# Splitting PSUM between exponentiated scores and maxima in a causal-attention kernel

## The chip, the cores and the metric

The kernel runs on one core of a Trainium2 chip. The metric is the device time of one execution in microseconds (us). A core has five engines that run side by side: TensorE (PE, matmuls; PEld is its loading of weights), VectorE (DVE), ScalarE (ACT), GpSimd (POOL) and SyncE (SP, which here issues most DMAs). Matmuls write to PSUM, which has 8 banks of 512 float32 columns by 128 partitions. "Bank" below is one of these, a "double bank" two in a row.

## What is computed

A transformer layer on 4096 tokens of width 256, in float32. Causal self-attention with 16 heads of 16 channels comes first, then three feed-forward blocks. All weights carry low-rank additions that the kernel folds in.

```python
qkv = lora_linear(x, w_attn, b_attn, la_attn, lb_attn)
q, k, v = jnp.split(qkv, 3, axis=2)
...
att = jnp.einsum('bhqd,bhkd->bhqk', q, k) * (1.0 / np.sqrt(HD))
causal = jnp.tril(jnp.ones((Tlen, Tlen), dtype=bool))
att = jnp.where(causal[None, None], att, -jnp.inf)
att = jax.nn.softmax(att, axis=-1)
y = jnp.einsum('bhqk,bhkd->bhqd', att, v)
y = y.transpose(0, 2, 1, 3).reshape(Bsz, Tlen, Cdim)
return lora_linear(y, w_proj, b_proj, la_proj, lb_proj)
```

The softmax subtracts each row's own maximum, so the kernel computes scores twice: once with queries on the partitions, to find the maxima, and once with keys on the partitions, to exponentiate them.

## The kernel before

*Tiling.* The 4096 tokens are 8 chunks (`ch`) of 512. The 16 heads are 4 groups (`g`) of 4. The attention works through 32 pairs `(ch, g)` in order, each called a group here: the queries of one chunk, four heads, and all the keys up to that chunk. Keys go in tiles `kt` of 128, four to a chunk.

*A use.* `uses_of` (L580) lists the steps of a group. One use is one key tile for one pair of the four heads. A chunk's own four key tiles lie on the diagonal and are packed in 5 uses; the earlier ones give 8 uses a chunk. So a group has 5 + 8 ch uses, from 5 to 61, and there are 1056 in all, 896 of them off the diagonal. `scores` (L603) does one use. It takes a double bank, one bank for each head of the pair. Two matmuls (L611), on 64 rows of the array each, write the scores, and two more (L620) add the negative maxima of the queries. ScalarE exponentiates the double bank into the tile `probs` (L628), and for tiles on the diagonal GpSimd sets what is masked to zero (L631).

*Values.* `values` (L642) multiplies probabilities and values: for each of the four heads a matmul of 32 output rows into the bank `av` (L653). `pieces_of` (L589) cuts this work: off the diagonal a piece is one key tile with one half of the 512 queries, so there are as many pieces as uses. In the profile each of these float32 matmuls appears as two, so that a piece shows as eight. After the last piece ScalarE copies `av` out (L662), and `finish` (L664) transposes it, divides by the sums and stores it in `y`.

*Maxima.* `maxima_of` (L504) makes the maxima of one group in as many steps as it has uses. A step takes a double bank, one bank a head, filled by two matmuls (L524). Off the diagonal one reduction on VectorE (L533) takes both banks, 1024 columns, and gives two maxima a row. On the diagonal VectorE adds a mask and takes the maximum for each head and query tile (L538, each with a read of the accumulator). When all parts are there, three small operations give the group's maxima, and `spread_maxima` (L565) transposes them and copies them to `ms` (L574), which L620 reads.

*PSUM.* Three double banks `ps_sc`, shared by scores to be exponentiated and by maxima; one bank `ps_m` for everything else (`misc()`, L108: projections, transposes, folds of weights; while the kernel is starting, these too take from `ps_sc`); and one bank `av`.

*Order.* Each engine runs its instructions in the order in which the code issues them (`manual_schedule`). The loop at L868 goes through all groups and uses, and each use issues: `scores`; the maxima steps that are due; the piece of values that lies two uses back (`behind`); and then one of `finish` of the group before (at use 2), `spread_maxima` of the group after (third last use), or some steps of the generators `others`. These are `prep` (L444), which normalizes, transposes and projects a chunk two chunks ahead and writes its queries and keys to DRAM, and the preparation of weights for the tail. The maxima run a group ahead: those of group n + 1 are due evenly over the uses of group n, all `LEAD` = 5 uses early (L822 to L826). A group whose successor belongs to the next chunk therefore makes 8 maxima steps more than it has uses.

*Keys and queries* come back from DRAM by `fetch` (L435), stacked as the scores want them: 12 buffers `ks` (one holds a chunk's keys for a group) and 3 `qs`. SP's queue issues these in order, and each waits until its buffer is free.

*The tail.* When the attention is done, all pools but the constants are freed, and the output projection, the residuals and the feed-forward blocks of the 8 chunks run in an order written out by hand (`ORDER`, L46). The change does not touch it.

Of the kernel before, what the change touches and what calls it, by code (L numbers as in the profile page):

```python
# [43 lines left out]
LEAD = 5  # L44
# [8 lines left out]
def tile_layer(  # L53
# [48 lines left out]
    ps_m = until_phase_two("ps_m", bufs=1, space=PSUM)  # L102
    ps_sc = until_phase_two("ps_sc", bufs=3, space=PSUM)
    ps_av = until_phase_two("ps_av", bufs=1, space=PSUM)

    starting = True

    def misc():  # L108

        if starting:  # L110
            return ps_sc.tile([P, 2, 512], F32, tag="sc", name="misc")[:, 0, :]
        return ps_m.tile([P, 512], F32, tag="misc", name="misc")
# [84 lines left out]
    w_stack = work.tile([P, NC, 2, 2 * P], F32, tag="p", name="w_stack", bufs=4)  # L197
# [210 lines left out]
    def stack(xnT, i, pair, t):  # L408
# [3 lines left out]
        for c in range(NC):  # L412
# [7 lines left out]
        high = prepared.tile([P, CH], F32R, tag="half0", name="half0", bufs=3)  # L420
# [3 lines left out]
            high, ps, AF.Identity, bias=b_low[:, at : at + 1], scale=is_low[:, i : i + 1]  # L424
        )
        nc.vector.scalar_tensor_tensor(
            t[:, pair, :],
            ps,
            b_stack[:, at : at + 1],
            high.bitcast(F32),  # L430
# [13 lines left out]
    def prep(ch):  # L444
# [20 lines left out]
        for f in range(NC):  # L465
# [3 lines left out]
            if ch == f == 0:  # L469
# [3 lines left out]
                    for tag, bufs in (("qs", 3), ("ks", 12))  # L473
                )
                kss[0, 0] = {0: k0}
                qss[0, 1], kss[0, 1] = fetch("qs", qds[0], 1, 3), {0: fetch("ks", kds[0], 1, 12)}
# [27 lines left out]
    def maxima_of(ch, g):  # L504
# [4 lines left out]
        for kc in [ch, *range(ch)]:  # L509
            if kc not in ks:  # L510
                ks[kc] = fetch("ks", kds[kc], g, 12)
# [7 lines left out]
            for use in uses:  # L519
                ps = ps_sc.tile([P, 2, 512], F32, tag="sc", name="sc_max")  # L520
                for t, pair, at, w in use:
                    for i in range(2):
                        rows = ds(64 * i, 64)
                        nc.tensor.matmul(  # L524
                            ps[:, i, ds(at, w)],
# [5 lines left out]
                for t, pair, at, w in use:  # L531
                    if kc < ch:
                        nc.vector.tensor_reduce(  # L533
                            parts[:, t, 2 * pair : 2 * pair + 2, kc], ps, AX.X, ALU.max
                        )
                    for i in range(2 if kc == ch else 0):
# [3 lines left out]
                            in0=ps[:, i, ds(at, w)],  # L540
# [5 lines left out]
                            accum_out=parts[:, t, 2 * pair + i, kc : kc + 1],  # L546
# [42 lines left out]
    def pieces_of(ch):  # L589

        own, half = NT * ch, CH // 2
        pieces = [[], [(own, 0, CH)], [(own + 1, half, CH)]]
        pieces += [[(own + 1, P, half), (own + 3, 3 * P, CH)], [(own + 2, half, CH)]]
        return pieces + [[(kt, a, a + half)] for kt in range(own) for a in (0, half)]
# [6 lines left out]
    def scores(ch, g, use):  # L603
# [23 lines left out]
        pr = work.tile([P, 2, CH], F32, tag="p", name="probs", bufs=4)  # L627
# [14 lines left out]
    def values(ch, g, piece):  # L642
# [5 lines left out]
        for kt, lo, hi in pieces[piece]:  # L648
            for j in range(4):
# [4 lines left out]
                    av[ts(j, 32), lo:hi],  # L654
                    lhsT=vs[kt // NT][:, kt % NT, ds((4 * g + j) * VW, 32)],
                    rhs=pr[:, j % 2, lo + shift : hi + shift],
                    start=kt == NT * ch,
# [172 lines left out]
    with tc.manual_schedule(engines=computing):  # L830
        made = 0

        def maxima_until(turn):
            nonlocal made
            while made < len(dues) and dues[made] <= turn:
                next(stream)
                made += 1
# [26 lines left out]
        starting = False  # L864
        spread_maxima(0, 0)

        behind = []
        for n, (ch, g) in enumerate(groups):  # L868
            uses = uses_of(ch)
            if g == 0:  # L870


                others, count, done = iter(()), 0, 0
                turns = (G - 1) * len(uses) - 2 * LEAD
                if ch == 0:
                    others, count, turns = chain(following, late), 12, G * len(uses)
                if ch + 2 < NCH:
                    others, count = chain(others, prep(ch + 2)), count + 12
                if ch < 2 * NB:
                    weights = ffn_weight(ch)  # L880
                    if ch:
                        next(weights)
# [77 lines left out]
```

## Time and profile before

| | us |
|---|---|
| median of 3 runs (lowest, highest) | 2104.53 (2104.1, 2105.01) |
| the profiled execution | 2102.8 |
| its span, first to last instruction | 2100.8 |
| first exponential starts | 50.4 |
| last exponential starts | 1834.5 |

Groups of a chunk, from the start of a group's first exponential to that of the next group's (the last one: to the start of the last exponential), in us:

| ch | uses | g = 0 | 1 | 2 | 3 |
|---|---|---|---|---|---|
| 0 | 5 | 33.5 | 19.1 | 36.0 | 19.9 |
| 1 | 13 | 25.2 | 32.0 | 28.5 | 23.5 |
| 2 | 21 | 34.0 | 42.2 | 40.1 | 35.7 |
| 3 | 29 | 45.9 | 54.8 | 51.7 | 47.1 |
| 4 | 37 | 57.6 | 65.2 | 65.3 | 58.9 |
| 5 | 45 | 69.4 | 76.9 | 76.5 | 71.4 |
| 6 | 53 | 80.2 | 80.2 | 82.1 | 82.8 |
| 7 | 61 | 91.6 | 91.7 | 89.9 | 75.1 |

Reading the profile: a line names an engine, a line of the code and an operation, with what it writes `<-` what it reads. In groups, "busy, mean" is the time that the group's instructions cover together (us) and the mean of one (ns), and after the bar stands how long the engine was idle just before them and what ended that. In the timeline, a line starts with its start and its length in us; the bracket at the end has the idle time before it and what released it. In sums by stretch, the columns are the stretch, its length, then busy time and count of PE, PEld, DVE, ACT and POOL, the granted clock of TensorE, the DMA share and GB/s. In the page's slices, each digit is the busy share of one fortieth of the span, in tenths. The chain of waits is the work that ended last, followed back; its lines have start and length.

### The profile page before, as it was taken

How to read it: one execution, taken by the hardware profiler on the slowest of the kernel's cores; microseconds unless marked ns; L12 is line 12 of the kernel's file. 1: busy time of each engine (PE TensorE's matmuls, PEld its weight loads, DVE VectorE, ACT ScalarE, POOL GpSimd, SP SyncE). 2: the span in 40 equal slices, each digit the busy share in tenths (PEclk: the TensorE clock that was granted, in tenths of full speed). 3: DMA queues.
4: the chain of work that ended last, by engine and by line, in shares of the span. 5: the costliest groups of instructions: out<-in, count | busy, mean ns of one | idle time of the engine just before them, and what ended most of it. 6: DMA issues, size and time to landing. Idle time of an engine off the chain costs nothing.

```text
span 2100.8 us, 41401 instructions
## 1 busy us (share of the span) xinstructions
PE 2004.6 (95%) x17150; PEld 1002.0 (48%) x17150; DVE 1607.7 (77%) x2706; ACT 1311.1 (62%) x1458; POOL 221.8 (11%) x538
## 2 busy tenths in 40 slices
PE   7679999999999999999999999999999999999996
PEld 4344444444444444444444444444444444377764
DVE  4557887987798778887788888888888883078666
ACT  2336576676667666676666666666676677855544
POOL 1111110010100000000000000000000001033223
PEclk9889999999999999999999999999999999999998
DMA  5534224124121321212211211111211101020002
GB/s 175 204 133 162 84 88 131 57 85 131 57 72 51 106 72 53 71 60 96 78 51 41 72 51 51 58 54 41 71 41 61 51 31 71 2 100 1 1 1 80
DMA packets 85984, 152.26 MB, mean 72 GB/s; under 512 B 6938, under 2 KB 22787, under 8 KB 85796
## 3 DMA queue, kind: packets, MB, share of 16 engines
q1 hardware_dynamic: 84148, 145.29, 20.8%
q0 software_dynamic: 1008, 3.67, 0.5%
q8 instruction: 134, 2.20, 0.4%
q10 hardware_dynamic: 640, 0.66, 0.1%
q14 instruction: 54, 0.44, 0.1%
HBM read 107.66 MB, written 41.94 MB: 71 GB/s over the span
## 4 chain that ended last, share of the span: by engine, by line
PE 79%; DVE 14%; ACT 3%; issue 2%; DMA 1%; SPq 0%; POOL 0%; ACTq 0%; DVEq 0%; POOLq 0%
PE av L653 24%; PE sc_exp L611 19%; PE sc_max L524 11%; PE sc_exp L620 10%; DVE masked L538 8%; PE ps L706 4%; PE ps L777 3%; PE misc L386 3%; DVE parts L533 2%; PE misc L489 1%; PE ps L698 1%; DVE st L344 1%; ACT probs L628 1%; PE misc L669 1%; DMA kd<-half 1%
## 5 line engine op out<-in xcount | busy, mean ns | idle before, releaser
L628 ACT ACTIVATE probs<-sc_exp 128x1024 f32<-128x1024 f32 x1056 | 1082.3, 1025 | 492.1 <-PE sc_exp L620 462.1
L533 DVE TENSOR_REDUCE parts<-sc_max 128x2 f32<-128x1024 f32 x896 | 1083.7, 1224 | 197.1 <-PE sc_max L524 195.0
L653 PE MATMUL av<-probs,v 128*32 128x256 f32 (+2 forms) x8448 | 670.1, 392 | 0.2 <-ACT probs L628 0.2
L611 PE MATMUL sc_exp<-qs,ks 64*128 64x512 f32 (+3 forms) x2304 | 544.9, 471 | 18.2 <-DVE parts L538 16.5
L524 PE MATMUL sc_max<-ks,qs 64*128 64x512 f32 (+3 forms) x2304 | 429.2, 386 | 25.6 <-DVE parts L538 8.3
L620 PE MATMUL sc_exp<-ms,ones 64*128 64x512 f32 (+3 forms) x2304 | 430.5, 376 | 0.2 <-ACT ms L574 0.2
L611 PEld LDWEIGHTS sc_exp<-qs,ks 64*128 64x128 f32 x2304 | 215.9, 184 | 449.9 <-issue 300.9
L653 PEld LDWEIGHTS av<-probs,v 128*32 128x32 f32 x8448 | 169.1, 108 | 276.1 <-issue 240.2
L524 PEld LDWEIGHTS sc_max<-ks,qs 64*128 64x128 f32 x2304 | 213.7, 185 | 169.2 <-ACT probs L628 48.9
L538 DVE CUSTOM_DVE_ANT_0 masked<-sc_max,mask 128x384 f32<-128x384 f32 (+3 forms) x512 | 251.0, 490 | 51.4 <-PE sc_max L524 24.6
L631 POOL TENSOR_SCALAR_AFFINE_SELECT probs<-probs 128x256 f32<-128x256 f32 x256 | 99.8, 408 | 1576.6 <-ACT probs L628 1576.6
L620 PEld LDWEIGHTS sc_exp<-ms,ones 64*128 64x128 f32 x2304 | 219.9, 187 | 0.6 <-ACT ms L574 0.6
L706 PE MATMUL ps<-w_f,hT 128*128 128x256 f32 x384 | 86.1, 380 | 1.0 <-ACT u L356 0.8
L777 PE MATMUL ps<-fm,w_f 128*128 128x512 f32 x192 | 86.0, 594 | 0.5 <-DVE u L734 0.3
L706 PEld LDWEIGHTS ps<-w_f,hT 128*128 128x128 f32 x384 | 71.9, 190 | 13.4 <-issue 2.4
L386 PE MATMUL misc<-xnT,w_qkv 128*128 128x512 f32 x128 | 66.4, 645 | 7.1 <-DVE half L395 6.3
L395 DVE SCALAR_TENSOR_TENSOR half<-misc,b_all,half 128x512 fp32r<-128x512 f32 x32 | 24.0, 750 | 63.2 <-ACT half L394 63.2
L672 DVE RECIPROCAL rden<-misc 128x16 f32<-128x16 f32 x32 | 7.9, 248 | 83.9 <-PE misc L669 83.9
L356 ACT ACTIVATE u<-u,shift,rstd 128x256 f32<-128x256 f32 x96 | 49.0, 592 | 27.9 <-POOL shift L352 24.6
L766 ACT ACTIVATE fm<-ps,f_vecs 128x512 f32<-128x512 f32 x48 | 34.1, 776 | 44.3 <-PE ps L698 44.3
L394 ACT ACTIVATE half<-misc,b_all 128x512 fp32r<-128x512 f32 x32 | 22.0, 688 | 62.8 <-PE misc L386 61.1
L777 PEld LDWEIGHTS ps<-fm,w_f 128*128 128x128 f32 x192 | 35.5, 190 | 38.5 <-issue 35.4
(102 smaller groups left out, 942.8 us busy)
## 6 DMA issues: line engine op xcount, KB each, us to landing
ks<-kd SPq DMA_DIRECT2D x143, 512.0 KB
qd<-half SPq DMA_DIRECT2D x64, 256.0 KB
kd<-half SPq DMA_DIRECT2D x64, 256.0 KB
qs<-qd SPq DMA_DIRECT2D x31, 512.0 KB
x_sb<-in_x_dram SPq DMA_DIRECT2D x8, 512.0 KB
yd<-y SPq DMA_DIRECT2D x8, 512.0 KB
xt<-in_x_dram SPq DMA_DIRECT2D x8, 512.0 KB
out_dram<-u SPq DMA_DIRECT2D x8, 512.0 KB
```

Of the source, the lines that this page charges most:

```text
L356: nc.scalar.activation(dst[:, t, :], src[:, t, :], AF.Identity, bias=shift[:, t : t + 1], scale=rstd[:, t : t + 1],)
L386: nc.tensor.matmul(ps, lhsT=w_qkv[:, c, ds(i * C + f * P, P)], rhs=xnT[:, c, :], start=c == 0, stop=c == NC - 1,)
L524: nc.tensor.matmul(ps[:, i, ds(at, w)], lhsT=qs[rows, pair, ts(t, P)], rhs=ks[kc][rows, pair, :w], start=True, stop=True,)
L533: nc.vector.tensor_reduce(parts[:, t, 2 * pair : 2 * pair + 2, kc], ps, AX.X, ALU.max)
L538: nc.vector.tensor_tensor_reduce(out=masked[:, :w], in0=ps[:, i, ds(at, w)], in1=mask[:, CH - w :], scale=1.0, scalar=NEG, op0=ALU.add, op ...
L611: nc.tensor.matmul(ps[:, i, ds(at, CH - c0)], lhsT=ks[kt // NT][rows, pair, ts(kt % NT, P)], rhs=qs[rows, pair, c0:], start=True, stop=False,)
L620: nc.tensor.matmul(ps[:, i, ds(at, CH - c0)], lhsT=ones[rows, pair, :], rhs=ms[rows, c0:], start=False, stop=True,)
L628: nc.scalar.activation(pr, ps, AF.Exp, scale=SM_SCALE)
L631: nc.gpsimd.affine_select(out=pr[:, :, ds(at, P)], in_=pr[:, :, ds(at, P)], pattern=[[0, 2], [1, P]], compare_op=ALU.is_ge, fill=0.0, base ...
L653: nc.tensor.matmul(av[ts(j, 32), lo:hi], lhsT=vs[kt // NT][:, kt % NT, ds((4 * g + j) * VW, 32)], rhs=pr[:, j % 2, lo + shift : hi + shift ...
L706: nc.tensor.matmul(ps[:, t, :], lhsT=srcT[:, c, ts(t, P)], rhs=w[:, c, :], start=c == 0, stop=c == NC - 1,)
L777: nc.tensor.matmul(ps[:, o, :], lhsT=w_f[2 * b + 1][:, c, ts(o, P)], rhs=gT[:, c, :], start=c == 0, stop=c == NC - 1,)
```

## The change

- PSUM is dealt out anew: `ps_sc` has two double banks, for scores to be exponentiated alone; `ps_m` has three single banks, and `misc()` takes from these always, from the start on. `av` keeps its bank.
- A maxima step takes two single banks, one a head. Off the diagonal it now has two reductions of 512 columns where it had one of 1024. On the diagonal the reductions are the same, in order of head.
- A piece of values is a key tile with all 512 queries (or all that the diagonal leaves), and becomes ready with the last use that its `probs` come from.
- The loop goes in turns of two uses, across the ends of groups: scores of both uses; maxima due by the first; the pieces that were ready before this turn; maxima due by the second; then, for each use, `finish`, `spread_maxima` or `others`. `spread_maxima` comes one use earlier (fourth last), `finish` at use 3.
- `LEAD` is 6, `probs` has 5 buffers, `ks` has 11. `stack` writes its first result where the second will stand, not in a buffer `half0`.

```diff
-LEAD = 5
+LEAD = 6
...
-    ps_m = until_phase_two("ps_m", bufs=1, space=PSUM)
-    ps_sc = until_phase_two("ps_sc", bufs=3, space=PSUM)
+    ps_m = until_phase_two("ps_m", bufs=3, space=PSUM)
+    ps_sc = until_phase_two("ps_sc", bufs=2, space=PSUM)
...
-    def misc():
-
-        if starting:
-            return ps_sc.tile([P, 2, 512], F32, tag="sc", name="misc")[:, 0, :]
-        return ps_m.tile([P, 512], F32, tag="misc", name="misc")
+    def misc(name="misc"):
+        return ps_m.tile([P, 512], F32, tag="one", name=name)
...
-        high = prepared.tile([P, CH], F32R, tag="half0", name="half0", bufs=3)
+        dst = t[:, pair, :]
...
-                ks[kc] = fetch("ks", kds[kc], g, 12)
+                ks[kc] = fetch("ks", kds[kc], g, 11)
...
-                ps = ps_sc.tile([P, 2, 512], F32, tag="sc", name="sc_max")
+                pss = [misc("sc_max") for _ in range(2)]
                 for t, pair, at, w in use:
                     for i in range(2):
                         rows = ds(64 * i, 64)
                         nc.tensor.matmul(
-                            ps[:, i, ds(at, w)],
+                            pss[i][:, ds(at, w)],
...
-                for t, pair, at, w in use:
-                    if kc < ch:
-                        nc.vector.tensor_reduce(
-                            parts[:, t, 2 * pair : 2 * pair + 2, kc], ps, AX.X, ALU.max
-                        )
-                    for i in range(2 if kc == ch else 0):
+                for i, ps in enumerate(pss):
+                    for t, pair, at, w in use:
+                        part = parts[:, t, 2 * pair + i, kc : kc + 1]
+                        if kc < ch:
+                            nc.vector.tensor_reduce(part, ps, AX.X, ALU.max)
+                            continue
...
-        own, half = NT * ch, CH // 2
-        pieces = [[], [(own, 0, CH)], [(own + 1, half, CH)]]
-        pieces += [[(own + 1, P, half), (own + 3, 3 * P, CH)], [(own + 2, half, CH)]]
-        return pieces + [[(kt, a, a + half)] for kt in range(own) for a in (0, half)]
+        own = NT * ch
+        return [[own], [own + 1, own + 3], [own + 2], *([kt] for kt in range(own))]
...
-        pr = work.tile([P, 2, CH], F32, tag="p", name="probs", bufs=4)
+        pr = work.tile([P, 2, CH], F32, tag="p", name="probs", bufs=5)
...
-                    av[ts(j, 32), lo:hi],
+                    av[ts(j, 32), c0:],
                     lhsT=vs[kt // NT][:, kt % NT, ds((4 * g + j) * VW, 32)],
-                    rhs=pr[:, j % 2, lo + shift : hi + shift],
-                    start=kt == NT * ch,
+                    rhs=pr[:, j % 2, c0 + shift : CH + shift],
+                    start=piece == 0,
...
-            for i, use in enumerate(uses):
-                scores(ch, g, use)
-                maxima_until(begin[n] + i)
-                if len(behind) == 2:
-                    values(*behind.pop(0))
-                behind.append((ch, g, i))
-                if n and i == 2:
-                    finish(*groups[n - 1])
-                elif i == max(3, len(uses) - 3) and n + 1 < len(groups):
-                    spread_maxima(*groups[n + 1])
+        for turn in range(0, len(every), 2):
+            ready = len(behind)
+            for n, i in every[turn : turn + 2]:
+                ch, g = groups[n]
+                uses = uses_of(ch)
+                scores(ch, g, uses[i])
+
+                for piece, kts in enumerate(pieces_of(ch)):
+                    last = max(j for j, use in enumerate(uses) if any(k[0] in kts for k in use))
+                    if last == i:
+                        behind.append((ch, g, piece))
+            maxima_until(turn)
+            for piece in behind[:ready]:
+                values(*piece)
+            del behind[:ready]
+            maxima_until(turn + 1)
+            for n, i in every[turn : turn + 2]:
+                ch, g = groups[n]
+                size = len(uses_of(ch))
+                if g == i == 0:
+                    others, count, until = others_of(ch)
+                    done = 0
+                if i == max(3, size - 4) and n + 1 < len(groups):
+                    spread_maxima(*groups[n + 1])
+                if i == 3 and n:
+                    finish(*groups[n - 1])
+                if i != 3 and i != size - 4:
...
```

`others_of` computes the same steps and counts as the lines that stood in the loop.

## The prediction

> **What bounds the kernel now.** I read the page's engine shares and slices first, then the sums by stretch for single groups, then the timeline of one use, and last the groups by shape and the chain.
>
> ```profile
> PE 2004.6 (95%) x17150; PEld 1002.0 (48%) x17150; DVE 1607.7 (77%) x2706; ACT 1311.1 (62%) x1458; POOL 221.8 (11%) x538
> PE   7679999999999999999999999999999999999996
> DVE  4557887987798778887788888888888883078666
> ```
>
> TensorE is full from the fourth slice to the end of the attention, VectorE is next, in the same slices at eight to nine tenths. The tail (from 1834 us) is untouched by the change. One group each, in us (busy time and count per engine):
>
> ```profile
> 1160.90:1241.00 80.10, 79.23 (x770) 36.09 (x768) 67.66 (x86) 55.35 (x55) 3.12 (x8) 1.00 0.18 60
> 1403.30:1486.20 82.90, 82.30 (x784) 37.40 (x782) 73.95 (x88) 55.53 (x56) 3.12 (x8) 1.00 0.16 52
> 1759.40:1834.50 75.10, 74.73 (x740) 28.97 (x736) 0.68 (x2) 62.04 (x62) 6.97 (x15) 1.00 0.14 50
> ```
>
> These are the first and last group of chunk 6 (53 uses) and the very last group (61 uses, no maxima left to make). PE, third column, fills each; VectorE (fifth) has 12.4, 9.0 and 74 us free. The granted clock is 1.00. One use:
>
> ```profile
> 1502.10 0.64 PE L653 MATMUL av<-probs,v 128*32 128x256 f32 x8
> 1502.21 1.23 DVE L533 TENSOR_REDUCE parts<-sc_max 128x2 f32<-128x1024 f32 x1 [0.23 <-PE sc_max L524]
> 1502.67 0.49 PE L611 MATMUL sc_exp<-qs,ks 64*128 64x512 f32 x2
> ...
> 1503.01 0.40 PE L620 MATMUL sc_exp<-ms,ones 64*128 64x512 f32 x2
> ...
> 1503.24 0.40 PE L524 MATMUL sc_max<-ks,qs 64*128 64x512 f32 x2
> 1503.50 1.02 ACT L628 ACTIVATE probs<-sc_exp 128x1024 f32<-128x1024 f32 x1 [0.43 <-PE sc_exp L620]
> ...
> 1503.57 0.64 PE L653 MATMUL av<-probs,v 128*32 128x256 f32 x8
> ```
>
> Start to start on PE: L611 0.34, L620 0.23, L524 0.33, L653 0.57, together **1.463 us a use**, with no wait. Steps that follow one of the same tiling (64 rows) cost 0.23; a change between it and the 32-column tiling costs 0.1 more on either side. VectorE works 1.23 and idles 0.23; ScalarE works 1.02 and idles 0.43.
>
> **The change part by part.** *Prices.* These rows give them (busy, mean ns):
>
> ```profile
> L533 DVE TENSOR_REDUCE parts<-sc_max 128x2 f32<-128x1024 f32 x896 | 1083.7, 1224 | 197.1 <-PE sc_max L524 195.0
> L653 PE MATMUL av<-probs,v 128*32 128x256 f32 x7680 | 614.3, 391 | 0.2 <-ACT probs L628 0.2
> L538 DVE CUSTOM_DVE_ANT_0 masked<-sc_max,mask 128x512 f32<-128x512 f32 x128 | 88.2, 689 | 20.3 <-PE sc_max L524 14.2
> L653 PE MATMUL av<-probs,v 128*32 128x512 f32 x256 | 34.3, 608 | 0.0
> ```
>
> *Values.* 7680 matmuls of 256 columns become half as many of 512. Eight of 256 take 0.57 to the next step: 0.24 for the first four, 0.33 for the others and the change of tiling. Eight of 512 start their second four after 0.45 (timeline at 1408.49), and the rest grows by 608 - 391 = 217 ns to 0.54: 1.00 us in place of 2 x 0.57.
>
> *Turns of two.* Order per turn: L611, L620, L611, L620, maxima A, values, maxima B. PE alone: four scores at 0.235 (the first now follows maxima B, the same tiling), A 0.325, values 1.00, B 0.333: **2.59 us against 2.93**.
>
> *Maxima in halves.* 896 reductions of 1024 columns become 1792 of 512. The masked rows (689, 557, 424, 291 ns for 512 to 128 columns) and L533's 1224 all lie on 157 ns + 1.04 ns a column, so a half takes 0.69 alone. Back to back they overlap:
>
> ```profile
> 1402.38 2.37 DVE L533 TENSOR_REDUCE parts<-sc_max 128x2 f32<-128x1024 f32 x2
> ```
>
> Two take 2.37, so the second costs 1.145, 0.08 less. A half in a row then costs 0.61, a step's pair 1.22, a turn 2.45 (no overlap: 2.76; all of the fixed cost hidden: 2.13). That fits under 2.59, with little left.
> The Trainium skill ("VectorE: DVE Perf Modes", The DRAIN you can't avoid) says that the next operation does not start until the pipe is empty, which speaks against the change: by it a turn's halves cost 4 x 0.69 = 2.76, and the sum would be that of the second rival. The 2.37 of this trace shows 0.08 of overlap, and I keep the trace's value.
>
> *The new wait.* A turn takes four single banks of a ring of three. So the second matmul of A needs the bank that the first half of the turn before's B leaves. That makes a loop: matmuls of B 0.50 (they load weights unhidden, as L611's 497 against L620's 392) and 0.04 to VectorE, half 0.69, 0.05 back, matmul of A to the values 0.43 (0.325 + the 0.105 of the unhidden load), values 1.00: **2.71 us a turn**. Behind that matmul on PE stand the values, B and the next scores, and so the exponentials. I take 2.71, as it is a sum of rows; the ends are 2.59 (the wait is hidden) and 2.93 (nothing gained). Scores' own two banks do not bind: 0.24 + 0.5 + 1.02 + 0.05 = 1.8 us a bank, and ScalarE needs 2.05 a turn. So: 840 full uses = 420 turns x (2.93 - 2.71) = **-92**. In the last group PE needs 2.12 a turn and ScalarE 2.05; at 2.17 it takes 66 of 75.1: **-9**.
>
> *Own steps of a group* (5 of them, masked, VectorE 7.8 to 9.2 us from L538's 251 + 42 us over 32 groups, take 8.4). Chunk 6's group spends 80.1 - 48 x 1.463 = 10.0 us there, with finish and spread. After, VectorE bounds it: 8.4 + 1.4 (L672, L675 and the group's small steps) = 9.8. **0**.
>
> *Last group of a chunk.* It makes the next chunk's maxima: 8 steps more than it has uses. VectorE then needs 9.8 + 8(ch+1) x 1.22, above the 10 + 8ch x 1.355 of the turns by 9.8 - 1.1 ch: 46 us over chunks 0 to 6. Before, the eight cost PE 0.23 each, which VectorE's gaps hid (82.9 against 80.1 and 80.3): about 1.9 x 7 = 13 are already in the time. **+33**.
>
> *Other PSUM steps.* Projections and the like had one bank in turn:
>
> ```profile
> 139.84 2.00 PE misc L386 x4
> ...
> 141.86 0.70 ACT half L394
> ...
> 142.58 0.76 DVE half L395
> ...
> 143.38 1.99 PE misc L489 x8
> ```
>
> PE stood 1.5 us for the two that empty the bank. With three banks the next can start. Chunk 0 has a dozen such places, some with scores between: **-8** (0 to -20). Later a single such tile in the ring must wait for a half (0.1 us) and delays the one three takes later; some 130 of them (finish, spread, preparation) at 0 to 0.2: **+5**. The setup before 50 us gives maxima two of the three banks where they took one: within that +5.
>
> *At nothing:* `ks` 12 to 11 buffers. In chunk 7 a tile is needed 10 uses (13.5 us) after its buffer is free, and a fetch took 3.6 us (chain at 55.31) to 7.8 (`qs`, at 100.19). If that cover goes, SP's queue stands and the maxima wait, as they did once for 4.6 us. `probs` 4 to 5 holds what a turn more needs. Writing `stack` in place saves a buffer, same instructions. LEAD 6 shifts when steps are due, not how many.
>
> **Sum.** -92 - 9 + 0 + 33 - 8 + 5 = -71. The profiled execution took 2102.8 (span 2100.8): 2031.8; the median of the runs is 1.7 above it: **2033 us**.
>
> **Rivals.** *PE alone* (the loop does not bind, halves hide more): 420 x 0.333 = -140, last group -9, chunk ends 9.8 - 0.6 ch, 56 - 13 = +43, others -3: 1995. For it: the loop exceeds PE by only 0.12. Against: it has no slack, and any VectorE step between adds.
> *No overlap of halves*: a pair 1.38, a turn 2.78: -61 - 9, chunk ends 11 each, 77 - 13 = +64, -3: 2095. For it: each half is a new instruction with its own release. Against: the 2.37 above.
> *VectorE becomes the bound* (the other side): with a pair p, 840 p - 1229 for the turns, 56 p - 13 for chunk ends, -12 for the rest; zero at p = 1.40, a half of **0.70 us in a row**. At 0.75, +90: 2195. For it: 0.69 alone is close, and VectorE is at 85% now. Against: PE's halves are ready together, so nothing need hold the second.
> *It doesn't do what it says*: the built order shows 1920 value matmuls of 512 columns and two maxima steps a turn, so no.
>
> **How the numbers follow.** Forecast 0.42 (2005 to 2060), PE alone 0.18 (1970 to 2005), no overlap 0.15 (2060 to 2100), within 0.2% (what can be told from no change) 0.03, VectorE or the ring as the bound 0.22. Faster 0.75, same 0.03, slower 0.22. Range 1980 to 2125: it takes in the ends of the turn's price, less the outermost 0.05 below and 0.14 above.
>
> **What would show it.** L653 in 512 columns, about 1.0 us a block; a full turn of 2.6 to 2.75; L533 halves of 0.69, pitch 0.61; PE's wait before maxima A released by VectorE's L533; chunk-end groups with VectorE at 95% or more; the last group at 66 us. Wrong: a pitch of 0.70 or more, turns near 2.9, or exponentials waiting for their two banks.

## The result, and the profile after

The changed kernel takes **2095.41 us** (median of 6 runs, 2092.06 to 2098.62) against 2104.32 for the kernel before, run beside it on the same chip: a ratio of 0.996 (95% interval 0.9948 to 0.9973). So it is faster by 9 us, where 71 were forecast. The profiled execution took 2095.48 us, with a span of 2093.8.

The page of the changed kernel, engine shares and slices:

```profile
PE 1967.8 (94%) x13310; PEld 1060.3 (51%) x13310; DVE 1644.6 (79%) x3602; ACT 1253.0 (60%) x1458; POOL 221.1 (11%) x538
PE   7678999999999999999999999999999999999996
DVE  4455787798789878998888999999999994078666
PEclk9768999999999999999999999999999999999998
```

TensorE is busy for 37 us less than before, and VectorE for 37 more; VectorE now has nines from the 23rd slice to the 33rd; after that no maxima are left to make. The third and fourth slices of the clock read 6 and 8 where the kernel before had 8 and 9. Groups as before, from first exponential to first exponential, in us:

| ch | g = 0 | 1 | 2 | 3 | chunk, after | chunk, before |
|---|---|---|---|---|---|---|
| 0 | 26.9 | 51.5 | 20.4 | 35.2 | 134.0 | 108.5 |
| 1 | 28.6 | 35.0 | 28.7 | 26.7 | 119.0 | 109.2 |
| 2 | 33.5 | 47.2 | 38.5 | 40.2 | 159.4 | 152.1 |
| 3 | 44.3 | 55.8 | 50.1 | 50.9 | 201.1 | 199.4 |
| 4 | 54.8 | 66.8 | 60.3 | 61.5 | 243.5 | 247.1 |
| 5 | 65.7 | 75.0 | 72.0 | 74.0 | 286.6 | 294.2 |
| 6 | 74.0 | 77.0 | 76.1 | 84.8 | 311.9 | 325.3 |
| 7 | 84.8 | 87.8 | 82.0 | 68.4 | 323.0 | 348.3 |

The loss sits in the first chunks, where a group has few steps off the diagonal, and the gain in the last. Groups g = 1 and 3 begin in the middle of a turn, so that what they show is some 3 us more than what g = 0 and 2 show for the same work (in chunk 6, 77.0 against 74.0); a chunk's sum is free of this.

One full turn of the changed kernel, from its timeline (start, length):

```profile
1541.63 0.50 PE L521 MATMUL sc_max<-ks,qs 64*128 64x512 f32 x2
...
1541.96 0.39 PE L604 MATMUL sc_exp<-qs,ks 64*128 64x512 f32 x2
...
1542.16 2.48 DVE L532 TENSOR_REDUCE parts<-sc_max 128x1 f32<-128x512 f32 x4 [0.22 <-PE sc_max L521]
...
1542.88 0.52 PE L521 MATMUL sc_max<-ks,qs 64*128 64x512 f32 x2
...
1543.33 1.06 PE L647 MATMUL av<-probs,v 128*32 128x512 f32 x8
...
1544.33 0.50 PE L521 MATMUL sc_max<-ks,qs 64*128 64x512 f32 x2
```

From maxima B (1541.63) to the next maxima B (1544.33) are **2.70 us**; 2.71 were forecast. Values take 1.00 to the next start, as forecast, and four halves in a row take 2.48, a pitch of 0.60 after a first of 0.69 (forecast 0.61). The groups and the waits name the same things:

```profile
L532 DVE TENSOR_REDUCE parts<-sc_max 128x1 f32<-128x512 f32 x1792 | 1117.3, 682 | 124.3 <-PE sc_max L521 113.7
L647 PE MATMUL av<-probs,v 128*32 128x512 f32 x3840 | 515.4, 608 | 0.0
```

```profile
PEld sc_max L521 <- DVE parts L532: 356.8, 495, 1.5
```

This wait (us in total, times, longest) is that of the ring of three single banks: the weights of a maxima matmul are loaded only when a bank is free. It was 11.1 us in 42 waits before. So in a full turn the change did what the sum said. Sums by stretch show where it did not, first chunks 0 and 1 in the kernel before, then stretches of the changed kernel:

```profile
50.40:268.10 217.70, 182.57 (x1400) 96.55 (x1396) 148.96 (x403) 102.85 (x123) 32.28 (x82) 0.91 0.43 144
...
48.50:301.50 253.00, 205.10 (x1222) 110.43 (x1218) 154.66 (x457) 98.46 (x123) 32.17 (x82) 0.83 0.35 120
1192.10:1266.10 74.00, 73.03 (x558) 38.37 (x555) 67.74 (x129) 52.51 (x56) 3.11 (x8) 1.00 0.17 61
1419.10:1504.00 84.90, 81.97 (x596) 41.56 (x595) 77.61 (x149) 52.57 (x57) 3.11 (x8) 1.00 0.17 55
1758.60:1827.00 68.40, 68.40 (x520) 24.64 (x512) 0.68 (x2) 58.59 (x62) 6.96 (x15) 1.00 0.19 70
```

Those of the changed kernel are chunks 0 and 1, the first and last group of chunk 6, and the last group. Chunks 0 and 1 took 217.7 us before, with PE idle for 35 of them and a clock of 0.91; now PE is idle for 48 us of 253 and its clock is 0.83, so that 13 of the 35 us lost there are more idle time of PE and 22 are more busy time. The last group fell from 75.1 to 68.4 (forecast 66). Chunks 2 to 7 together went from 1566.4 to 1525.5: 41 us less. In them the forecast's terms (turns and last group, the later chunk ends, a few ring delays) come to some -75.

### The profile page after: what moved, and what is told of

Its sections match the earlier page's. It is cut to its first block, busy times and chain, and to the rows that moved or that the text cites. A ratio compares the mean times of both kernels' runs of the same rounds, so it can differ in the third digit from the quotient of the medians.

```text
span 2093.8 us, 34805 instructions
## 1 busy us (share of the span) xinstructions
PE 1967.8 (94%) x13310; PEld 1060.3 (51%) x13310; DVE 1644.6 (79%) x3602; ACT 1253.0 (60%) x1458; POOL 221.1 (11%) x538
## 4 chain that ended last, share of the span: by engine, by line
PE 75%; DVE 20%; issue 2%; ACT 1%; DMA 1%; POOL 0%; DVEq 0%; SPq 0%; ACTq 0%; POOLq 0%
PE av L647 22%; PE sc_max L521 16%; PE sc_exp L604 11%; PE sc_exp L613 10%; DVE masked L535 10%; DVE parts L532 6%; PE ps L700 4%; PE ps L771 3%; PE misc L383 3%; PE misc L486 1%; DVE st L341 1%; PE ps L692 1%; PE misc L663 1%; DMA qs<-qd 1%; DVE mv L342 1%
## 5 line engine op out<-in xcount | busy, mean ns | idle before, releaser
L621 ACT ACTIVATE probs<-sc_exp 128x1024 f32<-128x1024 f32 x1056 | 1023.7, 1022 | 428.0 <-PE sc_exp L613 420.5
L532 DVE TENSOR_REDUCE parts<-sc_max 128x1 f32<-128x512 f32 x1792 | 1117.3, 682 | 124.3 <-PE sc_max L521 113.7
L521 PE MATMUL sc_max<-ks,qs 64*128 64x512 f32 (+3 forms) x2304 | 604.9, 449 | 65.0 <-DVE parts L535 21.4
L521 PEld LDWEIGHTS sc_max<-ks,qs 64*128 64x128 f32 x2304 | 308.4, 187 | 570.0 <-DVE parts L532 356.8
L647 PE MATMUL av<-probs,v 128*32 128x512 f32 (+3 forms) x4608 | 569.8, 574 | 0.0
L604 PE MATMUL sc_exp<-qs,ks 64*128 64x512 f32 (+3 forms) x2304 | 473.3, 392 | 3.0 <-ACT probs L621 3.0
L613 PE MATMUL sc_exp<-ms,ones 64*128 64x512 f32 (+3 forms) x2304 | 450.0, 376 | 0.2 <-ACT ms L571 0.2
L604 PEld LDWEIGHTS sc_exp<-qs,ks 64*128 64x128 f32 x2304 | 238.1, 186 | 88.5 <-ACT probs L621 37.2
L613 PEld LDWEIGHTS sc_exp<-ms,ones 64*128 64x128 f32 x2304 | 244.6, 187 | 34.3 <-ACT ms L571 0.8
L647 PEld LDWEIGHTS av<-probs,v 128*32 128x32 f32 x4608 | 96.0, 109 | 149.1 <-issue 140.6
L353 ACT ACTIVATE u<-u,shift,rstd 128x256 f32<-128x256 f32 x96 | 49.0, 592 | 27.8 <-POOL shift L349 24.5
L392 DVE SCALAR_TENSOR_TENSOR half<-misc,b_all,half 128x512 fp32r<-128x512 f32 x32 | 24.0, 751 | 50.1 <-ACT half L391 45.6
```

Source lines behind the costliest of these rows:

```text
L353: nc.scalar.activation(dst[:, t, :], src[:, t, :], AF.Identity, bias=shift[:, t : t + 1], scale=rstd[:, t : t + 1],)
L521: nc.tensor.matmul(pss[i][:, ds(at, w)], lhsT=qs[rows, pair, ts(t, P)], rhs=ks[kc][rows, pair, :w], start=True, stop=True,)
L532: nc.vector.tensor_reduce(part, ps, AX.X, ALU.max)
L604: nc.tensor.matmul(ps[:, i, ds(at, CH - c0)], lhsT=ks[kt // NT][rows, pair, ts(kt % NT, P)], rhs=qs[rows, pair, c0:], start=True, stop=False,)
L613: nc.tensor.matmul(ps[:, i, ds(at, CH - c0)], lhsT=ones[rows, pair, :], rhs=ms[rows, c0:], start=False, stop=True,)
L621: nc.scalar.activation(pr, ps, AF.Exp, scale=SM_SCALE)
```

## The experiments

My theory after the first look: the turn's price is right, and the missing 62 us are (a) early waits for queries, brought by LEAD 6, and (b) the masked steps at each group's end, which I had at nothing. Rivals: (c) turns with three maxima steps at chunk ends, (d) VectorE's total time as the bound there, (e) the split costs what the turns gain. Where "after" stands below as a base, each edit is made to the changed kernel. All ratios are against the kernel before.

### One use less of lead

```diff
-LEAD = 6
+LEAD = 5
```

> The changed kernel with LEAD 5 in place of 6, nothing else. Theory (early waits): chunks 0 and 1 lost 35 us (253.0 us from the first exponential of chunk 0 to that of chunk 2, 217.7 before), because in groups of 5 uses a lead of 6 asks for a fourth group's queries while only three buffers qs exist; three waits of PE on these fetches take 20.1 us and the clock falls to 0.73. With 5 the waits fall below 10 us, chunks 0 and 1 take 230 to 242, the whole 2075 to 2087. Rival (the projections, clumped at the end of a turn and sharing three banks with maxima, are what costs there): chunks 0 and 1 stay within 4 us of 253, the whole 2091 to 2100. Both: turns of chunk 7 stay at 2.70 us.

Measured: 2082.89 us, ratio 0.9905 (0.9888 to 0.9921), 12.5 us below the changed kernel. Chunks 0 and 1 took 243.1 (expected 230 to 242), the turn stayed at 2.70. The waits for queries fell from 20.1 us to 14.7, not below 10 as expected, and the longest is still 11.8:

```profile
PE sc_max L521 <- DMA qs<-qd: 14.7, 3, 11.8
```

Theory (a) has the right place, but LEAD alone is only part of it: with 5, as before the change, the waits are still longer than the 5.1 us of the kernel before. The fourth buffer is tried below.

### The turns without the split

The changed kernel with PSUM dealt out as before (three double banks shared, one for the rest) and one reduction of 1024 columns a step; turns and whole value tiles stay.

```diff
-    ps_m = until_phase_two("ps_m", bufs=3, space=PSUM)
-    ps_sc = until_phase_two("ps_sc", bufs=2, space=PSUM)
+    ps_m = until_phase_two("ps_m", bufs=1, space=PSUM)
+    ps_sc = until_phase_two("ps_sc", bufs=3, space=PSUM)
...
-                pss = [misc("sc_max") for _ in range(2)]
+                ps = ps_sc.tile([P, 2, 512], F32, tag="sc", name="sc_max")
...
```

> The changed kernel with the PSUM of before (three double banks for scores and maxima together, one single bank for the rest, one reduction of 1024 columns a maxima step), turns of two and whole value tiles kept. Theory (the split is what turns of two need; a bank that must come free in time sets the turn): the second maxima step must wait for the first to be reduced whole, so a loop of 0.54 + 1.22 + 0.05 + 0.43 + 1.00 = 3.2 us a turn; 2190 to 2250 in all. Rival (the halves and the ring of three only cost, the turns alone bring the gain): turns at 2.6 to 2.7 and VectorE freed, 2040 to 2090.

Measured: 2249.06 us, ratio 1.0689 (1.0673 to 1.0705). A turn takes 3.25 us. Its timeline:

```profile
1701.74 1.23 DVE L535 TENSOR_REDUCE parts<-sc_max 128x2 f32<-128x1024 f32 x1 [0.20 <-PE sc_max L526]
...
1703.02 0.50 PE L526 MATMUL sc_max<-ks,qs 64*128 64x512 f32 x2 [0.40 <-DVE parts L535]
...
1706.27 0.49 PE L526 MATMUL sc_max<-ks,qs 64*128 64x512 f32 x2 [0.41 <-DVE parts L535]
```

A turn takes four double banks of three: maxima A stand until the reduction of the turn before gives its bank back (1701.74 + 1.23), 0.4 us of idle PE each time with the load of the weights unhidden after it, and the values stand behind them. The turns need the split.

### The split without the turns

The kernel before (its order, LEAD 5, half pieces of values) with PSUM split and reductions in halves.

```diff
-    ps_m = until_phase_two("ps_m", bufs=1, space=PSUM)
-    ps_sc = until_phase_two("ps_sc", bufs=3, space=PSUM)
+    ps_m = until_phase_two("ps_m", bufs=3, space=PSUM)
+    ps_sc = until_phase_two("ps_sc", bufs=2, space=PSUM)
...
-                ps = ps_sc.tile([P, 2, 512], F32, tag="sc", name="sc_max")
+                pss = [misc("sc_max") for _ in range(2)]
...
```

> The kernel before with the split PSUM and halved reductions alone; order by single uses, half value pieces, LEAD 5, buffers as before. Theory (PSUM split alone brings nothing, PE's mode changes set the use): 1.46 us a use in chunk 7 as before, ends of chunks some us longer, 2098 to 2120. Rival (sharing three banks with the projections is what costs chunks 0 and 1): there 240 us or more where before has 217.7, 2122 to 2145 in all.

Measured: 2180.17 us, ratio 1.0362 (1.0346 to 1.0377). Both expectations missed: **the split alone costs 76 us**. Not in a use:

```profile
1570.76 0.40 PE L519 MATMUL sc_max<-ks,qs 64*128 64x512 f32 x2
...
1572.22 0.41 PE L519 MATMUL sc_max<-ks,qs 64*128 64x512 f32 x2
```

The use is 1.46 as before. The last group of chunk 6 and the first of chunk 7:

```profile
1469.70:1559.00 89.30, 86.61 (x783) 39.44 (x781) 78.38 (x143) 55.47 (x55) 3.12 (x8) 1.00 0.15 47
1559.00:1651.80 92.80, 92.67 (x881) 42.35 (x880) 81.02 (x150) 63.65 (x64) 3.11 (x8) 1.00 0.17 58
```

They took 82.8 and 91.6 before. Most of the cost, 73 us, lies in three places: 13 us in chunks 0 and 1 (231.1 against 217.7); 30 in the last groups of chunks 2 to 6, between 5.2 and 6.5 each, whatever the chunk; 30 in the other groups of chunks 2 to 7, 0.7 to 3.2 each, but nothing in the very last, which makes no maxima (75.1 in both). So what costs lies where groups and chunks end, before any turn is made, which fits (b) and (c), though neither was taken away here.

### Whole tiles or half tiles, in the same turns

```diff
+            for lo in range(c0, CH, CH // 2 if piece > 2 else CH):
+                hi = lo + CH // 2 if piece > 2 else CH
...
```

> The changed kernel with each value tile cut again in two halves of 256 queries, both in the same turn. Theory (the gain of a turn comes from fewer changes of the array's tiling, not from longer matmuls): two halves in a row stream on, 0.24 + 2 x 0.21 + 0.33 = 1.0 us, so a turn stays at 2.68 to 2.76 and the whole at 2092 to 2115. Rival (whole tiles carry it): 2 x 0.57 = 1.14 a turn, 2.84, and 2140 to 2160 in all.

Measured: 2094.43 us, ratio 0.9958 (0.9943 to 0.9973): the changed kernel's time. The turn stays at 2.70.

```profile
L647 PE MATMUL av<-probs,v 128*32 128x256 f32 x7424 | 502.8, 387 | 0.2 <-ACT probs L621 0.2
```

Twice as many matmuls of half the columns, with 387 ns in place of 608, do the same work in the same time. Whole tiles carry nothing of the gain. What is left is that there is one block of values in a turn, and so fewer changes of tiling, as the rows of the kernel before price them.

### Masks left out of the maxima, in both kernels

On the diagonal a plain reduction takes the place of the masked one, so that the maxima of diagonal tiles include scores that are masked out. The same edit in each kernel:

```diff
-                        masked = small.tile([P, CH], F32, tag="masked", name="masked", bufs=1)
-                        nc.vector.tensor_tensor_reduce(
...
+                        nc.vector.tensor_reduce(part, ps[:, ds(at, w)], AX.X, ALU.max)
```

After:

> The changed kernel with a plain reduction in place of the masked one on the diagonal, for the same columns; the maxima then include the masked scores of the 128 x 128 diagonal tiles. Theory (the masked steps of a group bind the end of each group with only three single banks to run ahead in): the five steps cost VectorE 4 x 0.61 + 4 x (0.48 + 0.21) + 4 x 0.35 = 6.6 us in place of 9.5, each group ends 2 to 2.7 us earlier, 2015 to 2045 in all; full turns stay at 2.70. Rival (the transposes of finish and spread_maxima and their bank set the end of a group): 2075 to 2095.

Measured: 2035.36 us, ratio 0.9673 (0.9655 to 0.9691), 60 us below the changed kernel. Before:

> The kernel before with a plain reduction in place of the masked one, same columns; the maxima then include the masked scores of the diagonal tiles. Control for the run above. Theory (before, three double banks and VectorE's gaps hid the masked steps): 2088 to 2104. Rival (the masked steps cost the same in both kernels): 2030 to 2060.

Measured: 2077.02 us, ratio 0.9868 (0.9854 to 0.9883), 27 us below the kernel before: between the two expectations. So the masked steps were not free before either; what the change adds to them is 60 - 27 = **33 us**, which is (b). In chunks 2 to 7 alone the same difference, by the first exponentials, is 45.6 - 21.2 = 24.4 us, 1.0 for each of their 24 groups. The mechanism stands in VectorE's timeline at a group's end, with the masks first (the changed kernel):

```profile
1580.41 0.68 DVE L535 CUSTOM_DVE_ANT_0 masked<-sc_max,mask 128x512 f32<-128x512 f32 x1
1581.02 0.08 DVE L535 DVE_READ_ACCUMULATOR2_ANT parts<- 128x1 f32 x1
1581.25 0.69 DVE L535 CUSTOM_DVE_ANT_0 masked<-sc_max,mask 128x512 f32<-128x512 f32 x1
...
1589.45 0.42 DVE L535 CUSTOM_DVE_ANT_0 masked<-sc_max,mask 128x256 f32<-128x256 f32 x1
1589.80 0.08 DVE L535 DVE_READ_ACCUMULATOR2_ANT parts<- 128x1 f32 x1
```

the same operations in the kernel before:

```profile
1569.93 0.68 DVE L538 CUSTOM_DVE_ANT_0 masked<-sc_max,mask 128x512 f32<-128x512 f32 x1
1570.54 0.08 DVE L538 DVE_READ_ACCUMULATOR2_ANT parts<- 128x1 f32 x1
1570.65 0.69 DVE L538 CUSTOM_DVE_ANT_0 masked<-sc_max,mask 128x512 f32<-128x512 f32 x1
1571.27 0.08 DVE L538 DVE_READ_ACCUMULATOR2_ANT parts<- 128x1 f32 x1
1571.50 0.69 DVE L538 CUSTOM_DVE_ANT_0 masked<-sc_max,mask 128x512 f32<-128x512 f32 x1
...
1578.78 0.08 DVE L538 DVE_READ_ACCUMULATOR2_ANT parts<- 128x1 f32 x1
```

and the changed kernel without masks (the experiment):

```profile
1525.26 1.42 DVE L531 TENSOR_REDUCE parts<-sc_max 128x1 f32<-128x384 f32 x4 [0.22 <-PE sc_max L521]
1527.22 4.04 DVE L531 TENSOR_REDUCE parts<-sc_max 128x1 f32<-128x384 f32 x10 [0.54 <-PE sc_max L521]
```

A masked operation of 512 columns has a pitch of 0.84 us after (1580.41 to 1581.25): 0.69 itself, then the read of the accumulator and a gap of 0.15. A plain half in a row has 0.60. Before, pitches of 0.72 and 0.85 alternate: the gap after the read is 0.03 when the next operation reads the other bank of the same tile, and 0.15 when it reads a new tile. After, each bank is a tile of its own, so that nine of the fifteen gaps in this row are long where four were. So the same 16 operations run without a pause from 1580.41 to 1589.88, **9.47 us**, where before they took 8.93 (1569.93 to 1578.86). With a ring of three, PE stands behind them. At the end of chunk 7's first group three turns, by the starts of their exponentials, take 4.62, 2.76 and 3.73 us with masks, 3.94, 2.59 and 2.77 without.

### Half the columns in a reduction

Off the diagonal each half reduces 256 of its 512 columns, so that the maxima leave out half of the keys there.

```diff
-                            nc.vector.tensor_reduce(part, ps, AX.X, ALU.max)
+                            nc.vector.tensor_reduce(part, ps[:, : CH // 2], AX.X, ALU.max)
```

> The changed kernel with each off-diagonal reduction over only the first 256 of its 512 columns; the maxima leave out half of the keys. Theory (a bank waited for sets the turn at 2.70, and VectorE the chunk ends): a half takes 0.42 alone, the loop 2.44, so PE alone sets the turn, 2.59 to 2.62; the four groups at chunk ends with 8 steps more lose their excess of 5 to 8 us each; 2005 to 2035 in all. Rival (2.70 is what PE needs): turns stay at 2.68 to 2.70, 2045 to 2075.

Measured: 2018.28 us, ratio 0.9592 (0.9578 to 0.9606). A full turn:

```profile
1540.43 0.49 PE L521 MATMUL sc_max<-ks,qs 64*128 64x512 f32 x2
...
1540.96 0.76 DVE L532 TENSOR_REDUCE parts<-sc_max 128x1 f32<-128x256 f32 x2 [0.67 <-PE sc_max L521]
...
1541.68 0.40 PE L521 MATMUL sc_max<-ks,qs 64*128 64x512 f32 x2
```

2.58 us from one maxima B to the next (1543.01), with no wait before maxima A: PE alone, whose price of 2.59 was worked out from rows of the kernel before. The loop through VectorE is thus what the other 0.12 us of the turn are. But turns with three maxima steps still took 3.58, a full microsecond more than a turn of two, though VectorE works for only 2.2 us of them, and the last group of chunk 6 is still 6.3 us above the second (7.8 in the changed kernel), where the expectation had this excess gone. In this run something else than VectorE's work holds such turns:

```profile
1373.09 0.62 PE L521 MATMUL sc_max<-ks,qs 64*128 64x512 f32 x3
1373.51 1.43 DVE L532 TENSOR_REDUCE parts<-sc_max 128x1 f32<-128x256 f32 x4 [0.39 <-PE sc_max L521]
...
1373.99 0.49 PE L521 MATMUL sc_max<-ks,qs 64*128 64x512 f32 x1 [0.28 <-DVE parts L532]
```

When two steps stand in one place of a turn (maxima A or B), the fourth matmul waits until a bank comes back: fill 0.44, half 0.42, 0.05 back, 0.91 us, near the 1.00 measured. In the changed kernel, where a half takes 0.69, two of the four stand so (the weights' 0.42 and 0.41 of waiting):

```profile
1431.26 3.68 DVE L532 TENSOR_REDUCE parts<-sc_max 128x1 f32<-128x512 f32 x6 [0.57 <-PE sc_max L521]
...
1431.98 1.72 PE L521 MATMUL sc_max<-ks,qs 64*128 64x512 f32 x4
1432.60 0.18 PEld L521 LDWEIGHTS sc_max<-ks,qs 64*128 64x128 f32 x1 [0.42 <-DVE parts L532]
1433.20 0.18 PEld L521 LDWEIGHTS sc_max<-ks,qs 64*128 64x128 f32 x1 [0.41 <-DVE parts L532]
```

Such a turn takes 3.9 us where one of two steps takes 2.70. Two accounts give this number. The turnover of a bank, 0.44 + 0.69 + 0.05, is 1.18 us more; two halves more on VectorE, 2 x 0.60, are 1.20. But here VectorE reduces the six halves in a row, for 3.68 of the 3.90, and pauses no longer than in a turn of two (2.48 of 2.70). So with whole halves VectorE's work, (d), fills these turns; the experiment with spaced steps below bears on it.

### A fourth buffer of queries

Room for it comes from the keys.

```diff
-                    for tag, bufs in (("qs", 3), ("ks", 11))
+                    for tag, bufs in (("qs", 4), ("ks", 10))
...
```

> The changed kernel (LEAD 6) with four buffers qs and ten ks in place of three and eleven. Theory (with a lead of 6 a fourth group's queries are wanted while only three buffers exist): PE's waits on fetches of queries fall from 20 us to below 8, chunks 0 and 1 take 235 to 243 in place of 253, 2076 to 2088 in all. Rival (the fetch stands behind the writes of projections on SP's queue, whatever the buffers): chunks 0 and 1 at 249 to 256, 2091 to 2100.

Measured: 2082.66 us, ratio 0.99 (0.9881 to 0.9919). Chunks 0 and 1:

```profile
46.10:278.40 232.30, 199.46 (x1220) 108.45 (x1218) 154.73 (x457) 98.50 (x123) 32.31 (x82) 0.87 0.39 132
```

232.3 us (expected 235 to 243), 21 less, with no wait for queries left. Part of that is given back: chunks 2 to 7 take 1535.2 us where they took 1525.5. PE's maxima now wait for keys, which they do nowhere in the changed kernel:

```profile
PE sc_max L521 <- DMA ks<-kd: 11.0, 4, 3.3
```

Three of the four, 7.7 us, stand at the end of chunk 6 and in chunk 7, so ten buffers of keys are too few there. (a) is worth some 21 us in chunks 0 and 1. What the changed kernel waits for, from its timeline:

```profile
75.79 5.54 SPq L403 DMA_DIRECT2D kd<-half  x4
81.44 1.13 SPq L435 DMA_DIRECT2D qs<-qd  x1
```

```profile
87.83 0.79 PE L521 MATMUL sc_max<-ks,qs 64*128 64x512 f32 x2 [12.70 <-DMA qs<-qd]
```

Groups of chunk 0 have 5 uses, and LEAD is 6, so that a fourth group's maxima are due while three hold the buffers of queries. Its fetch is issued at 81.44, when four stores of keys ahead of it in SP's queue are through, and PE, with nothing else in its order, stands for 12.7 us. With a fourth buffer two fetches go out in a row before those stores:

```profile
44.60 1.89 SPq L435 DMA_DIRECT2D qs<-qd  x2
```

The kernel before issued the same fetch at 76.43, hardly earlier, but the first maxima that read it ran only at 83.65, after projections, and PE did not wait for it. Its one wait for queries came with the next fetch, of 100.19:

```profile
108.08 1.65 PE L524 MATMUL sc_max<-ks,qs 64*128 64x512 f32 x8 [5.14 <-DMA qs<-qd]
```

### At most one maxima step in a place

From chunk 2 on, the third step of a turn stands between the scores of the two uses in place of beside another.

```diff
+                if spaced(turn) and n * 1000 + i == every[turn][0] * 1000 + every[turn][1]:
+                    step_if(made + 1 < len(dues) and dues[made + 1] <= turn)
...
-            maxima_until(turn)
+            if spaced(turn):
+                step_if(made < len(dues) and dues[made] <= turn)
...
```

> The changed kernel, from chunk 2 on with at most one maxima step in a place, a third one of a turn between the scores of its two uses. Theory (two steps in a row need four of three banks, so the second waits until the first is reduced: turns with three steps take 3.9 us, and 3.58 with halved reductions): the third step gets a bank without that wait, such turns take 3.2 to 3.6, the groups at the ends of chunks 2 to 6 lose 2 to 5 us each, 2074 to 2087 in all. Rival (VectorE has too much to do there, wherever the steps stand): turns of three stay at 3.8 to 3.9, 2091 to 2099.

Measured: 2095.31 us, ratio 0.9944 (0.9926 to 0.9963). Turns of three steps still take 3.89 to 3.9, so the theory that the place matters falls, and the rival, VectorE's work, has both of its numbers. One such turn, and the start of the next:

```profile
1444.94 3.68 DVE L532 TENSOR_REDUCE parts<-sc_max 128x1 f32<-128x512 f32 x6 [0.21 <-PE sc_max L521]
1448.83 2.49 DVE L532 TENSOR_REDUCE parts<-sc_max 128x1 f32<-128x512 f32 x4 [0.21 <-PE sc_max L521]
```

VectorE works without a break for 3.68 of 3.89 us, so no order of the steps could save more than the pause of 0.21. With the experiment on half the columns: two limits lie close together in these turns, VectorE's work at 3.9 and the wait for a bank at some 3.6. Taking the first away shows the second; whether spacing would help then, no run shows.

### The two costs taken away together

Plain reductions as above (the diagonal's masks are left out of the maxima); the space of the mask tiles gives four buffers of queries and keeps eleven of keys.

```diff
-                    for tag, bufs in (("qs", 3), ("ks", 11))
+                    for tag, bufs in (("qs", 4), ("ks", 11))
...
-                        nc.vector.tensor_tensor_reduce(
...
+                        nc.vector.tensor_reduce(part, ps[:, ds(at, w)], AX.X, ALU.max)
```

> The changed kernel with plain reductions on the diagonal (the maxima then include the masked scores of the diagonal tiles) and, in the space of the mask and the masked tile that this frees, four buffers qs beside eleven ks. Theory (two separate costs of the change: masked steps 60 us, early waits for queries 21 us, of which four qs with ten ks gave 13 back): they add up, 2010 to 2020, and no turn in chunk 7 waits for keys. Rival (they overlap, VectorE's masked steps being late because of the early waits): 2024 to 2034.

Measured: **2010.91 us**, ratio 0.955 (0.9536 to 0.9564), below both kernels. TensorE is busy for 1927.3 us of it, 96% of the span. Chunks 0 and 1 take 218.9. The two costs add up, as expected: 60 us off the changed kernel for the masks, and 24.5 more for the buffer, which costs no key buffer here. Beside the kernel before without its masks (2077.02) this is 66 us less, near the 71 that were forecast for the change. And with the steps spaced too:

> The two runs above together. Theory: the costs add, 1990 to 2008. Rival (with cheaper diagonal steps the third step of a turn has slack already): within 4 us of the run with plain reductions and four qs.

Measured: 2012.01 us, ratio 0.9553 (0.9539 to 0.9567), no different from the run without the spacing: the expectation that the costs add missed, and the rival's range holds.

## Why the prediction was right in sign and wrong in size

*Turns, -92: right.* The loop at 2.71 was measured at 2.70, and taking VectorE's half of it away gave PE's own 2.58 (2.59 worked out). The prices of the values, the half and its pitch all came out within 0.01 to 0.02 us. The Trainium skill ("VectorE: DVE Perf Modes", The DRAIN you can't avoid) says that the next operation doesn't start until the pipe is empty, and, in the same paragraph, that one that isn't held starts earlier; the prediction left the second half out. By the first half alone four halves of 0.69 would take 2.76. They took 2.48, as the pair of 2.37 in the trace before let expect, which fits the second.

*Last group, -9: near.* It came to -6.7: its turns alternate between 2.12 and 2.36, where 2.17 was taken.

*The step that failed: "Own steps of a group ... 0".* It said that VectorE bounds a group's own portion after the change, at 8.4 + 1.4 = 9.8 us, against 10.0 before. VectorE did become the bound, but its work was mis-sized twice. I took busy time (251 + 42 us over 32 groups, put at 8.4 a group), where the pitch from one masked operation to the next gives 8.9 in the trace before already. And I took the diagonal's reductions for unchanged, because the diff says so: in single banks five more of them have the long gap, which makes 9.5. With 0.66 for the group's own maxima and 0.67 for finish that is 10.8. Without masks, the portion beyond the full turns or uses is the same in both kernels in chunk 7 (8.7 us in both, mean of the first two groups); with them it is 10.7 against 9.7. That is 1.0 a group, and by the two kernels without masks 33 us in all 32. The longer gaps are 0.54 of it by the trace; no run took them away alone. The experiment on the split alone shows the same rise with the old order (1.2 in chunk 7), so it comes with the split, not with the turns.

*The other step that failed: "LEAD 6 shifts when steps are due, not how many", at nothing.* True, and not harmless: what is due earlier needs its queries earlier, and a buffer of `qs` for them. LEAD is not the whole of it, as 14.7 us of the waits stay with 5; what else brings them forward, the order of the turns perhaps, no run took apart. The prediction looked at how long a key buffer is free in chunk 7, not at what a fourth group in flight needs in chunk 0, where a group is 5 uses and LEAD is more than one. Waits for queries went from 5.1 us in one to 20.1 in three, and the fourth buffer gave 21 us back. Had I followed the fetch of queries through SP's queue, I would have seen the stores of keys ahead of it.

*Last group of a chunk, +33: near in total by luck, half right in reason.* I had VectorE's total over the group against PE's, which shrinks with the chunk (9.8 - 1.1 ch, 3.2 in chunk 6). Measured, a chunk end from chunk 4 on has five or six turns of 3.9, each 1.2 above a full turn: 6 to 7 us in every one of them, and the last group of chunk 6 is 7.8 above the second, which begins in the same half of a turn. Seven such ends would make some 46, the forecast's sum before the 13 that were in the time already, if the early ones cost as much, which no row shows. VectorE is the bound, but turn by turn (3.68 us of work in 3.90): what it idles in the turns of two can't be used for the steps of another turn, so over the group it is busy for only 77.61 of 84.90, and the excess doesn't shrink. Behind it stands the wait for a bank, which the run with half the columns shows.

*Other PSUM steps, -8, and ring delays, +5: right in kind.* In chunk 0 PE's idle time after projections whose bank VectorE empties fell from 7.9 us to 3.0. The ring's delays can't be told apart from the own portion.

*The rest.* 62 us were missing: 33 of the masked steps and 21 of the early waits make 54. The other 8 are not settled. Groups with preparation steps (g = 1 in chunks 2 to 5, where some turns take 4.8 us) are a candidate that no run took apart; such groups stood out before the change too (65.2 against 57.6 in chunk 4). One reading of the prediction is off without consequence: VectorE's slices in the kernel before are at seven to nine tenths, not eight to nine.

*The rivals.* "No overlap of halves" lies at 2095, the time that was measured, and is still wrong: the pitch is 0.60. The number was hit by other costs. "VectorE becomes the bound" asked for a pitch of 0.70 in a row; it holds nowhere off the diagonal, but on the diagonal the masked operation has 0.84, which the prediction had no row for in its terms although the trace before contains it (0.72 and 0.85).

## What to carry to other kernels

Price an engine's work by its pitch (start to start) wherever it may become the bound; busy time leaves out the gaps, and here a tile cut in two added 0.12 us of gap with every operation the same. When a ring of buffers is made smaller, work out the loop for the steady turn and then again for every stretch that uses more or slower steps than the turn does: the ends of groups and chunks paid back what the turns gained. Making work due earlier is a demand on every buffer that this work reads from, and the shortest group decides.

## What the runs showed of the hardware

- Two value blocks of 256 columns in a row take as long as one of 512 (turn 2.70 with either), though two of 256 with other tilings between them cost 0.57 each against 1.00 for one of 512. The Trainium skill ("TensorEngine Tiling (Array Packing)", Key Properties) says that changing the tiling mode drains TensorE. The rows fit that, though no run shows the drain itself: a step of 64 rows beside one of 32 columns starts its follower 0.1 us later than one beside its like (0.33 and 0.34 against 0.23).
- A masked reduction with its accumulator read takes 0.72 us from start to start for 512 columns when the next one reads the same PSUM tile, and 0.84 when it reads a new one; a plain half takes 0.60. The operation itself is 0.69 in each.
- The mean granted clock of chunks 0 and 1 was 0.91 before, 0.83 after and 0.87 with the fourth buffer of queries. Idle time of PE alone doesn't order these runs: it was 35 us of 217.7, 48 of 253.0 and 33 of 232.3, and the split alone, with 25 of 231.1, had 0.87. What sets the clock there stays open. It also varies from one execution to the next: the run with spaced steps, which has the same work in chunks 0 and 1, took 260.0 us there at 0.81 where the changed kernel took 253.0, so a figure for these two chunks from one profile is good to some 7 us.
